# Third layer's first two blocks gathered ahead, in the last attention unit of a four-layer kernel

## The chip, the cores and the metric

One core of a Trainium2 chip runs the whole program in one launch. The metric is device time in microseconds (us) of one execution; it is given as the median of several runs. A profile comes from one further execution, whose own time is named beside its span.

## The reference, cut to what matters

Two images of 256 channels and 64 x 64 pixels go through four layers, all in fp32:

- layer 0: group norm, then attention with 4 heads over the 4096 pixels, a projection, and the sum with the normalised input;
- layer 1: a position term, linear in the pixel's place, is added;
- layer 2: a bottleneck (1x1 convolution to 64 channels, a deformable 3x3 convolution with mask, 1x1 back to 256, residual, relu);
- layer 3: twice (group norm, relu, deformable 3x3 convolution of 256 channels whose offsets come from a 7x7 depthwise and a 1x1 convolution), and the residual.

A deformable convolution samples, for each pixel and each of 9 taps, the image at a place of its own:

```python
y0 = jnp.floor(py); x0 = jnp.floor(px)
out = gather(y0, x0) * (wy0 * wx0) + gather(y0, x0 + 1) * (wy0 * wx1) \
    + gather(y0 + 1, x0) * (wy1 * wx0) + gather(y0 + 1, x0 + 1) * (wy1 * wx1)
```

The text speaks of the "second layer" (the bottleneck, layer 2) and the "third layer" (the deformable pair, layer 3), as the program's names do.

## The kernel before, in words

**Tiling.** An image is cut into 8 blocks of 512 pixels (8 rows). Each engine but SyncE executes its instructions in the order in which the Python code emits them (`manual_schedule`), so the loops below are the schedule; SyncE's DMAs are ordered by the framework. Each engine, SyncE's queue too, is in order: an instruction that waits holds all behind it.

**Attention** (`attention`). Four units (image b, pair of heads hp), each of 256 steps `n`; 16 steps are a block of 256 query pixels, so there are 64 attention blocks. A step issues scores (L569), the minimum (L581), exponentials (L587), transposes (L599) and products with the values (L628). `Block` holds what follows a block: `product` copies the products to the tile `o` (L460, one buffer), `spread` sends the shares through DRAM (`share_d` L495, two loads `f` L499), `combine` multiplies and adds on POOL (L508, L509, L514), `fetch` loads `res` (L203) and `project` projects (L533), stores `xa` (L546). Tile pools: `xp` 4, `kp` 5, `vp` 6 buffers. Small work is run from `due` times and from generators in the list `back`; `background` lets a generator take a step when no due work stands there: `bott.before` (second layer: 1x1, image to DRAM, offsets, corner indices and weights), `bott.conv(0)` and `early_image` (batch 0 of the second layer, its group norm, its output `xn` and gather image `img3[0]` in DRAM). `bott.before(1)` runs in the last unit and ends after it.

**Gathers.** `gather` (L817) is an indirect DMA on POOL's queue: 128 indices fetch the four corners of 128 pixels for one tap, a row of 4 KB each for the third layer (`four`, 512 KB) and 1 KB for the second (`bfour`). `offsets` makes a block's offsets: 14 matmuls into `pd` (L777), a copy `wide` (L788), 7 shifted matmuls (L794), a copy `od` (L803), 4 selections (L808), and `corners` (L722 to L760), which makes the indices `idx` and the weights `w4`.

**Third layer** (`deform`). 4 passes (two images, two convolutions) of 8 blocks of 36 steps `s`, 1152 in all: step `s` is one tap `k` and one quarter `j` of a block's pixels. A step issues the gather of step s + 8 (ten buffers in `gp`), the first corner of step s + 1 on ScalarE (`first`, L1328), the other three on DVE (`others`, L1334, three instructions), two transposes (L1346), every fourth step an evacuation (L1355), and one of the products with the weights (L1365). `Side` objects run generators beside the steps, at so many calls a step: the offsets of the blocks to come (24 calls for 36 steps), the `image` of the next pass, and `seconds`, which is `bott.conv(1)`, the second layer's batch 1. That has 144 units of two gathers, two calls each (DVE: `weigh` L1020, `add` L1030 and L1031; transposes L1041, products L1051 and L1073, output L1076, L1082, L1083, store to `x2d` L1118); with 8 units gathered ahead and the last steps it is about 312 calls. It starts before step 0 with 20 calls and goes on at 312 / 180 = 1.73 calls a step. When it ends, the image of batch 1 starts at 1.15 calls a step.

Of the kernel before, what the change touches and what calls it, by code (L numbers as in the profile page):

```python
# [18 lines left out]
P = 128  # L19
# [5 lines left out]
EPS = 1e-5  # L25
DWK = 7


# [32 lines left out]
class Net:  # L61
    def __init__(self, ctx, tc, a, out):
# [23 lines left out]

        self.pos_d = dram.tile([C, HW], F32, name="pos_d")
        self.share_d = [dram.tile([16, P], F32, name=f"share_d{n}") for n in range(2)]

# [83 lines left out]
    def attention(self, bott):  # L173
# [5 lines left out]
        with ExitStack() as ctx:  # L179
# [20 lines left out]

            def block(src, i, pool=xp, name="xb"):
                t = pool.tile([P, 2, 512], F32, name=name)
                nc.sync.dma_start(t, rows(src)[:, :, 512 * i : 512 * i + 512])  # L203
                return t
# [185 lines left out]
            def plan_unit(u):  # L390
# [4 lines left out]
                def load(key, i, b):  # L395
                    x.setdefault(key, []).append(block(self.xn_d[b], i))

# [38 lines left out]
            class Block:  # L436
# [81 lines left out]
                def fetch(self):  # L518
                    b, hp = units[self.u]
                    i = self.i // 2  # L520
                    self.res = block((self.xn_d, self.xa_d)[hp][b], i, one, "res")
                    if hp == 0:
                        src = rows(Block.pos_d)[:, :, 512 * i : 512 * i + 512]
                        self.pos = one.tile([P, 2, 512], F32, name="pos")
                        nc.sync.dma_start(self.pos, src)
# [139 lines left out]
            while n < last + 4 or back or any(own.values()):  # L665
                u, d = divmod(n, per_unit)
                if d == 0 and u < len(units):
                    plan_unit(u)
                    if u == 0:
                        back.append(prepare(1))  # L670
                    if u == 1:
                        back.append(bott.before(0, bt, ps))
                    if u == 2:
                        back.append(first_batch())
                    if u == 3:
                        back.insert(0, bott.before(1, bt, ps))

                def small(at):
# [83 lines left out]

    def offsets(self, i, srcs, wt, bias, base, idx, w4, pool, ods, ps):

# [8 lines left out]
        for s, src in enumerate(srcs):  # L773
            for t in order:
# [4 lines left out]
                    lhsT=wt(s, t),  # L779
                    rhs=src[:, (y + r0) * W : (y + r1) * W],  # L780
                    start=(n == 0),
                    stop=(n == len(srcs) * size - 1),
                )
                n += 1
                yield

        wide = ods[i % 2]
        nc.scalar.copy(wide[:m, :, half : half + W], pd[:m].rearrange("p (r w) -> p r w", w=W))  # L788
        yield
        pz = ps([P, 512])  # L790
        sums = pz.rearrange("p (r w) -> p r w", w=W)
        for t in range(size):
# [7 lines left out]
            )  # L800
        yield
        od = pool.tile([P, 512], F32, name="od")
        nc.scalar.activation(od, pz, AF.Identity, bias=bias)  # L803
        yield

        pt = ps([P, 4, 32])
        for j in range(4):
            nc.tensor.matmul(  # L808
                pt[:, j, :], lhsT=od[:, j * P : (j + 1) * P], rhs=self.sel, start=True, stop=True
            )  # L810
        yield
        for _ in self.corners(i, pt, False, base, idx, w4, pool):
# [12 lines left out]
    class Bottleneck:  # L825
# [4 lines left out]
        GROUPS = [(0, 1), (2, 3), (4, 5), (6, 7), (8,)]  # L830
        CORNERS = 11

        def __init__(self, ctx, net):
# [3 lines left out]
            self.corner = ctx.enter_context(tc.tile_pool(name="bt_c", bufs=self.CORNERS))  # L837
            self.idx, self.w4 = {}, {}
            self.h, self.blocks, self.done = {}, [0] * B, set()
            self.w1 = wp.tile([P, 2, CM], F32, name="w1")  # L840
# [77 lines left out]
        def before(self, b, pools, ps):  # L918
# [20 lines left out]
            def offsets(i):  # L939
# [30 lines left out]
                for _ in range((1, 6)[b]):  # L970
                    yield False
                while len(self.idx) == self.CORNERS:
                    yield False
                pt = ps([P, 4, 32])
                for j in range(4):
# [6 lines left out]
                for _ in net.corners(i, pt, True, self.base, idx, w4, work):  # L982
                    yield "any"

            for i in range(NB):
# [143 lines left out]
    def early_image(self, bott, pools, ps):  # L1129
# [6 lines left out]
        for i in range(NB):  # L1136
# [11 lines left out]
            for g in range(2):  # L1148
# [15 lines left out]
                yield True  # L1164

    def deform(self, bott):

# [3 lines left out]
        tc, nc, a = self.tc, self.nc, self.a  # L1171
        with ExitStack() as ctx:
            wp = ctx.enter_context(tc.tile_pool(name="df_w", bufs=1))
            work = ctx.enter_context(tc.tile_pool(name="df_work", bufs=2))
            cp = ctx.enter_context(tc.tile_pool(name="df_c", bufs=4))
            gp = ctx.enter_context(tc.tile_pool(name="df_g", bufs=10))
            sp = ctx.enter_context(tc.tile_pool(name="df_s", bufs=8))
# [24 lines left out]
            def offset_weights(l):  # L1202
# [9 lines left out]
                for cb in range(2):  # L1212
                    nc.vector.tensor_tensor(
                        self.wf[:, cb],
                        dw[:, cb].unsqueeze(2).to_broadcast([P, T, 2 * K2]),
                        pw[:, cb].unsqueeze(1).to_broadcast([P, T, 2 * K2]),
                        ALU.mult,
                    )
                    yield
# [3 lines left out]
            def conv_weight(l, k):  # L1223

                src = a["dcw"][l].rearrange("(c p) o -> p c o", p=P)
                wc[k] = wp.tile([P, 2, C], F32, name=f"wc{k}")
                nc.sync.dma_start(wc[k], src[:, 2 * k : 2 * k + 2, :])

# [40 lines left out]
            IMAGE = 4 + 6 * NB + 1  # L1269
            corners = {}  # L1270

            def offsets(b, l):
                if b == 0:
                    yield from offset_weights(l)
                wf = self.wf
                for i in range(NB):
                    idx = cp.tile([P, 4, K2], I32, name="didx")
# [8 lines left out]
                        self.vec[:, V_PWB + l : V_PWB + l + 1],  # L1286
                        base, idx, w4, work, ods, pd,
                    )

            begun = offsets(0, 0)  # L1290
            next(begun)
            load(0, self.xn_d[0], wp)
            ods = [wp.tile([P, 8, W + DWK - 1], F32, name=f"wide{n}") for n in range(2)]
# [15 lines left out]
            def gather(s):  # L1309
                if s < ALL:  # L1310
                    n, i, k, j = parts(s)
                    b, l = layers[n]
                    fours[s] = gp.tile([P, 4, C], F32, name="four")
                    idx = corners[b, l, i][0]
                    self.gather(
                        fours[s].rearrange("p s c -> p (s c)"), self.img3[b], idx[:, j, k : k + 1]
                    )

# [87 lines left out]
            class Side:  # L1406


                def __init__(self, start, rate, steps):
                    self.start, self.rate, self.steps, self.count = start, rate, steps, 0  # L1410

                def follow(self, s):
                    while self.steps and self.count < self.rate * (s - self.start):
                        self.count += 1
# [7 lines left out]
            second = bott.conv(1, bott.pools(inner, 9), ps)  # L1422
            offs = [Side(-LEAD - 6, OFFS / BLOCK, begun)]
            for k in range(K2):
                conv_weight(0, k)
            for s in range(-LEAD - 6, 0):
                offs[0].follow(s + 1)
                if s % 3 == 0:
                    next(second)
            for s in range(AHEAD):  # L1430
                gather(s)
            first(0)

            seconds = Side(0, 312 / (5 * BLOCK), second)
            stats[0] = self.norm_stats()
            images = []
            for s in range(ALL + 12):
# [12 lines left out]
                if seconds:  # L1450
                    seconds.follow(s)
                    if not seconds.steps:
                        seconds = None
                        stats[1] = bott.stats[1]
                        inner.close()
                        images.append(Side(s, 1.15, image(*layers[1])))
                if s % LAYER == LAYER // 2 and 1 <= n < len(layers) - 1:
# [112 lines left out]
```

## Time and profile before

| | |
|---|---|
| median of 3 runs | 5334.04 us (5333.5 to 5345.14) |
| the profiled execution | 5333.18 us, span 5331.4 us |
| busy: PE, DVE, ACT, POOL | 4839.4, 4190.9, 2822.3, 2238.2 us (91, 79, 53, 42%) |
| DMA | 920.43 MB, mean 173 GB/s |
| last attention unit, its exponentials | 2207.2 to 2940.1 us |
| third layer, step 0 (L1328) | 3025.7 us |

Engines: PE is TensorE's matmuls, PEld its weight loads, DVE VectorE, ACT ScalarE, POOL GpSimd, SP SyncE. In a group's line stand the source line, engine, operation, tile written and tiles read, number of instructions, busy time and mean of one in ns, and behind a second bar the idle time before them with what ended it. "issue" means that the profile shows nothing that was waited for; "remote" and "another core or an unknown queue" mean that it names no releaser.

### The profile page before, as it was taken

To read this page: it belongs to the slowest core of one execution; us is meant where nothing else is said; L and a number is where in the kernel's file an instruction comes from. 1 tells how busy PE (TensorE), PEld (TensorE's weight loads), DVE (VectorE), ACT (ScalarE), POOL (GpSimd) and SP (SyncE) were. 2 spreads that over 40 slices of the span, in tenths; PEclk is the share of its full clock that TensorE was granted. 3 is DMA by queue.
4 is the path that set the end of the run, shared out by engine and by line. 5 is a ranking of instruction groups with operands and counts; after the bars stand their busy time and mean duration, and the time that the engine had idled before them with its cause. 6 is when DMAs were issued, how large, how long until landed. Compare 5 with 4: busy or idle time off the path is not lost.

```text
span 5331.4 us, 99714 instructions
## 1 busy us (share of the span) xinstructions
PE 4839.4 (91%) x38200; PEld 2655.5 (50%) x38200; DVE 4190.9 (79%) x7927; ACT 2822.3 (53%) x5221; POOL 2238.2 (42%) x2238
## 2 busy tenths in 40 slices
PE   8999999999999999999999655566999999999998
PEld 5555565555655555555565222233444444444443
DVE  6877868787678888687777466677999999999998
ACT  5676656666566666666677121223444444444443
POOL 0111101000027777461000566674566566666664
PEclk9999999999999999999999777788999999999999
DMA  5222121111213333233301566567999999999997
GB/s 170 63 89 61 41 69 35 49 29 45 61 55 94 96 94 103 85 97 103 92 25 35 185 189 203 185 201 249 356 315 333 351 350 348 341 386 344 346 347 286
DMA packets 347150, 920.43 MB, mean 173 GB/s; under 512 B 58717, under 2 KB 98459, under 8 KB 346671
## 3 DMA queue, kind: packets, MB, share of 16 engines
q0 software_dynamic: 194688, 683.85, 36.7%
q1 hardware_dynamic: 151438, 230.07, 14.0%
q8 instruction: 300, 4.92, 0.4%
q14 instruction: 180, 1.47, 0.1%
q10 hardware_dynamic: 544, 0.13, 0.0%
HBM read 815.90 MB, written 89.60 MB: 170 GB/s over the span
## 4 chain that ended last, share of the span: by engine, by line
PE 37%; DVE 13%; issue 6%; another core or an unknown queue 3%; ACT 3%; POOL 2%; DMA 2%; SPq 0%; DVEq 0%; ACTq 0%; POOLq 0%
PE out L1365 11%; DVE smp L1334 8%; PE pd L777 6%; PE av L628 5%; PE sc L569 5%; PE tt L599 3%; PE pt L1346 3%; POOL bfour L817 1%; DVE bfour L1020 1%; DVE low L581 1%; DMA four<-img,didx 1%; PE pd L794 1%; ACT st L1355 1%; ACT smp L1328 1%
## 5 line engine op out<-in xcount | busy, mean ns | idle before, releaser
L1334 DVE SCALAR_TENSOR_TENSOR smp<-four,dw,smp 128x256 f32<-128x256 f32 x3456 | 1611.6, 483 | 222.7 <-ACT smp L1328 94.6
L587 ACT ACTIVATE e<-sc,low 128x1024 f32<-128x1024 f32 x1024 | 1146.3, 1119 | 718.9 <-DVE low L581 700.5
L817 POOL DMA_INDIRECT four<-img,didx x1152 | 1153.2, 1001 | 723.6 <-DVE smp L1334 328.1
L1365 PE MATMUL out<-st,wc 128*128 128x512 f32 x2304 | 1239.8, 621 | 164.8 <-ACT st L1355 94.5
L581 DVE TENSOR_REDUCE low<-sc 128x1 f32<-128x1024 f32 x1024 | 1205.3, 1219 | 222.2 <-PE sc L569 212.9
L569 PE MATMUL sc<-k,qs 64*128 64x512 f32 x2048 | 997.5, 606 | 0.6 <-ACT e L587 0.3
L628 PE MATMUL av<-et,v 128*64 128x256 f32 x8192 | 994.9, 385 | 0.0
L569 PE MATMUL sc<-k,q 64*128 64x512 f32 x2048 | 978.9, 604 | 0.0
L508 POOL TENSOR_TENSOR o<-o,f 128x1024 f32<-128x1024 f32 x63 | 148.9, 2364 | 1863.6 <-DVE o L460 760.8
L599 PEld LDWEIGHTS tt<-ident,e 64*128 64x128 f32 x16384 | 651.3, 139 | 521.2 <-issue 270.2
L1355 ACT COPY st<-pt 128x1024 f32<-128x1024 f32 x288 | 291.2, 1011 | 930.5 <-PE pt L1346 627.9
L599 PE MATMUL tt<-ident,e 64*128 64x64 f32 x16384 | 727.3, 226 | 38.5 <-ACT et L618 23.4
L618 ACT COPY et<-tt 128x512 f32<-128x512 f32 x1152 | 658.2, 584 | 194.8 <-PE tt L599 164.3
L616 DVE COPY et<-tt 128x512 f32<-128x512 f32 x896 | 612.8, 684 | 153.5 <-PE tt L599 149.7
L1346 PEld LDWEIGHTS pt<-ident,smp 128*128 128x128 f32 x2304 | 320.1, 145 | 785.7 <-issue 489.3
L628 PEld LDWEIGHTS av<-et,v 128*64 128x64 f32 x8192 | 551.2, 137 | 304.0 <-issue 49.6
L817 POOL DMA_INDIRECT bfour<-img,bidx x576 | 577.4, 1002 | 269.7 <-issue 115.1
L1365 PEld LDWEIGHTS out<-st,wc 128*128 128x128 f32 x2304 | 393.3, 197 | 426.1 <-issue 273.4
L1346 PE MATMUL pt<-ident,smp 128*128 128x128 f32 x2304 | 460.0, 282 | 105.0 <-DVE smp L1334 81.7
L1328 ACT ACTIVATE smp<-four,dw 128x256 f32<-128x256 f32 x1152 | 512.8, 502 | 74.8 <-DMA four<-img,didx 55.2
L777 PE MATMUL pd<-x,wf 128*126 128x512 f32 (+2 forms) x896 | 455.5, 595 | 5.3 <-issue 5.0
L569 PEld LDWEIGHTS sc<-k,qs 64*128 64x128 f32 x2048 | 345.9, 188 | 218.3 <-issue 125.6
(165 smaller groups left out, 3353.4 us busy)
## 6 DMA issues: line engine op xcount, KB each, us to landing
f<-share_d SPq DMA_DIRECT2D x128, 256.0 KB
xb<-xn SPq DMA_DIRECT2D x55, 512.0 KB
img<-imgt SPq DMA_DIRECT2D x96, 256.0 KB
four<-img,didx POOLq DMA_INDIRECT x1152
xa<-res SPq DMA_DIRECT2D x32, 512.0 KB
xb<-in_x SPq DMA_DIRECT2D x20, 512.0 KB
bfour<-img,bidx POOLq DMA_INDIRECT x576
qs<-q SPq DMA_DIRECT2D x64, 128.0 KB
```

The source lines that it names most:

```text
L569: nc.tensor.matmul(s[:, j, :], lhsT=q[u, i // 2][int(h != j)][halves[j], at : at + P], rhs=k[u][c][halves[j], h, :], start=True, stop=True,)
L581: nc.vector.tensor_reduce(low, s, AX.X, ALU.max, negate=True)
L587: nc.scalar.activation(e.rearrange("p j n -> p (j n)"), s, AF.Exp, bias=blk.low[:, g, c : c + 1], accum_out=blk.sum[:, g, c : c + 1],)
L599: nc.tensor.transpose(pt[:, m, :], e[half, m // 4, m % 4 * P : m % 4 * P + P], self.ident[half, half],)
L616: nc.vector.tensor_copy(dst, pt)
L618: nc.scalar.copy(dst, pt)
L628: nc.tensor.matmul(now["av"][halves[h], :], lhsT=v[u][c][:, m, halves[h]], rhs=ets[j][:, m, h, :], start=(m == 0), stop=(m == 7),)
L777: nc.tensor.matmul(pd[:m, r0 * W : r1 * W], lhsT=wt(s, t), rhs=src[:, (y + r0) * W : (y + r1) * W], start=(n == 0), stop=(n == len(srcs) * ...
L817: self.nc.gpsimd.indirect_dma_start(out=dst, out_offset=None, in_=img, in_offset=bass.IndirectOffsetOnAxis(ap=idx, axis=0),)
L1334: nc.vector.scalar_tensor_tensor(smps[s], four[:, c], weight(s, c), smps[s], ALU.mult, ALU.add)
L1346: nc.tensor.transpose(pts[u][:, c, j * P : (j + 1) * P], smp[:, c * P : c * P + P], self.ident,)
L1365: nc.tensor.matmul(outs[ob], lhsT=wc[k][:, c, ob * P : ob * P + P], rhs=sts[u][:, c, :], start=(k == 0 and c == 0), stop=(k == K2 - 1 and ...
```

## The change

The offsets of the third layer's blocks 0 and 1 (first image, first convolution) are made by a new generator, `early_samples`, which is appended to `back` in the last attention unit. It takes buffers of the attention's pools (three of `xp` for the gathers; the fourth is handed to the attention's own loads through `held`; two of `vp` for rows of `xn`, one of `kp` for `wide`), makes the offsets with `offsets`, issues the 72 gathers, and stores each result from SyncE to a DRAM tile `samp_d`. In `offsets` the steps that fill a PSUM bank yield `"bank"`, on which `early_samples` goes on at once. A flag `bott.lock` keeps the corners of `before(1)` and of `early_samples` apart. In `deform` the first 72 steps load `four` from `samp_d`, steps 0 to 7 from POOL's queue and the others from SyncE; the first convolution's weights are loaded from POOL's queue; `gp` is allocated first. The second layer's 20 calls before step 0 go; `seconds` now has 0.9 calls a step and 2.5 more in each of the first 72 steps, and the image that follows it 0.9 in place of 1.15. The offsets' `Side` starts 72 steps later, with block 2.

```diff
+EARLY = 2
...
-    def offsets(self, i, srcs, wt, bias, base, idx, w4, pool, ods, ps):
+    def offsets(self, i, srcs, wt, bias, base, idx, w4, pool, wide, ps, odp=None, y0=0, later=lambda f: f()):
...
-                yield
+                yield "bank"
...
                     if u == 3:
                         back.insert(0, bott.before(1, bt, ps))
+                        back.append(self.early_samples(bott, bt, held, xp, vp, kp, ps))
...
-                while len(self.idx) == self.CORNERS:
+                while self.lock or len(self.idx) == self.CORNERS:
                     yield False
+                self.lock = True
...
+    def early_samples(self, bott, pools, held, xp, vp, kp, ps):
+        nc, a = self.nc, self.a
+        T, half = DWK * DWK, DWK // 2
+        xs = [vp.tile([P, 8, P], F32, name="v").rearrange("p m c -> p (m c)") for _ in range(2)]
+        src = self.xn_d[0].rearrange("(cb p) n -> p cb n", p=P)
...
+        xbs = [xp.tile([P, 2, 512], F32, name="xb") for _ in range(4)]
+        held.append(xbs.pop())
...
+        fours = deque(x.rearrange("p u n -> p (u n)") for x in xbs)
+        gathers, stores = deque(), deque()
+
+        def gather():
+            if stores:
+                nc.sync.dma_start(*stores.popleft())
+            if gathers:
+                dst, idx = gathers.popleft()
+                fours.rotate(1)
+                self.gather(fours[0], self.img3[0], idx)
+                stores.append((dst, fours[0]))
+
+        for i in range(EARLY):
...
+            for done in steps:
+                if done == "bank":
+                    continue
+                while bott.lock and not mine:
+                    yield False
+                bott.lock = mine = True
+                gather()
+                yield True
+            bott.lock = False
+            if i + 1 < EARLY:
+                load(i + 1)
+            while gathers:
+                gather()
+                yield True
+            for m in range(4 * K2):
+                k, j = divmod(m, 4)
+                gathers.append((self.samp_d[i][m * P : m * P + P, :], idx[:, j, k : k + 1]))
+        while gathers or stores:
+            gather()
+            yield True
...
+            gp = ctx.enter_context(tc.tile_pool(name="df_g", bufs=10))
             wp = ctx.enter_context(tc.tile_pool(name="df_w", bufs=1))
...
-                nc.sync.dma_start(wc[k], src[:, 2 * k : 2 * k + 2, :])
+                queue = (nc.gpsimd, nc.sync)[l]
+                queue.dma_start(wc[k], src[:, 2 * k : 2 * k + 2, :])
...
+                    if n == 0 and i < EARLY:
+                        queue = nc.gpsimd if s < AHEAD else nc.sync
+                        m = 4 * k + j
+                        queue.dma_start(four, self.samp_d[i][m * P : m * P + P, :])
+                        return
...
-                    while self.steps and self.count < self.rate * (s - self.start):
+                    while self.steps and self.count < self.rate * (s - self.start) + self.more(s):
...
-            offs = [Side(-LEAD - 6, OFFS / BLOCK, begun)]
-            for k in range(K2):
-                conv_weight(0, k)
-            for s in range(-LEAD - 6, 0):
-                offs[0].follow(s + 1)
-                if s % 3 == 0:
-                    next(second)
             for s in range(AHEAD):
                 gather(s)
+                conv_weight(0, s)
+            conv_weight(0, AHEAD)
+            begun = offsets(0, 0)
+            next(begun)
+            load(0, self.xn_d[0], wp)
+            offs = [Side(EARLY * BLOCK - LEAD - 6, OFFS / BLOCK, begun)]
             first(0)
 
-            seconds = Side(0, 312 / (5 * BLOCK), second)
+            seconds = Side(0, 0.9, second, lambda s: 2.5 * min(s, EARLY * BLOCK))
...
-                        images.append(Side(s, 1.15, image(*layers[1])))
+                        images.append(Side(s, 0.9, image(*layers[1])))
```

## The prediction

> **What bounds the kernel now.** I read the busy tenths of the 40 slices first, then the busy time by stretches, then the groups of instructions of the slow stretch, what one line of it did in time, and at last the chain of waits at the stretch's start and SyncE's timeline in the attention.
>
> ```profile
> PE   8999999999999999999999655566999999999998
> DVE  6877868787678888687777466677999999999998
> ...
> POOL 0111101000027777461000566674566566666664
> PEclk9999999999999999999999777788999999999999
> ```
>
> A slice is 133 us. From slice 23 to 28 (some 2950 to 3700 us) TensorE falls to half, its clock too, and POOL is at its highest. This is where the second layer's batch 1 runs beside the third layer's first blocks.
>
> ```profile
> 2599.70:2898.40 298.70, 297.32 (x3279) 178.93 (x3279) 220.10 (x348) 210.29 (x396) 30.48 (x21) 1.00 0.11 32
> ...
> 3011.00:3322.00 311.00, 167.54 (x523) 73.16 (x523) 199.18 (x469) 64.00 (x120) 215.96 (x213) 0.76 0.63 201
> 3322.00:3670.00 348.00, 207.18 (x672) 94.85 (x671) 239.86 (x555) 81.89 (x154) 231.09 (x225) 0.78 0.61 195
> ...
> 3848.00:5086.00 1238.00, 1174.19 (x4212) 570.97 (x4211) 1140.89 (x2690) 559.31 (x1043) 749.89 (x754) 0.99 0.95 345
> ```
>
> Columns: stretch, length, busy PE, PEld, DVE, ACT, POOL, clock, DMA share, GB/s. The last attention unit (first row) is TensorE's: 297 of 299 us, POOL idle, DMA at 0.11. The slow stretch (rows two and three) has no full engine: POOL 447 of 659, DVE 439. In the last row TensorE, DVE and DMA are all above 0.9: no room there.
>
> ```profile
> L817 POOL DMA_INDIRECT bfour<-img,bidx x288 | 293.4, 1019 | 184.4 <-issue 73.3 <-DVE bsmp L1031 58.4 <-DVE pos L731 20.0
> L1334 DVE SCALAR_TENSOR_TENSOR smp<-four,dw,smp 128x256 f32<-128x256 f32 x459 | 222.1, 484 | 100.2 <-ACT smp L1328 56.7 <-issue 14.4 <-ACT bst L1043 7.1
> ...
> L817 POOL DMA_INDIRECT four<-img,didx x162 | 166.3, 1026 | 49.4 <-issue 45.7 <-ACT smp L1328 1.8 <-ACT bst L1043 0.6
> ...
> L1020 DVE TENSOR_TENSOR bfour<-bfour,bw 128x512 f32<-128x512 f32 x137 | 93.7, 684 | 0.3 <-issue 0.3
> ...
> L1030 DVE TENSOR_TENSOR bfour<-bfour 128x256 f32<-128x256 f32 x137 | 57.6, 421 | 4.1 <-remote 1.7 <-DVE bfour L1020 0.7
> ...
> L1031 DVE TENSOR_TENSOR bsmp<-bfour 128x128 f32<-128x128 f32 x136 | 39.8, 293 | 20.3 <-remote 7.0 <-issue 2.2 <-DVE bfour L1030 1.5
> ...
> L1328 ACT ACTIVATE smp<-four,dw x162: 490/506/532, 3025.7 to 3660.1; 128x256 f32<-128x256 f32 x162
> ```
>
> A gather holds POOL for 1.02 us, and the next starts 0.30 us after it for "issue" (45.7/150): 1.32 us each. From the first gather after the start-up (3010.5) to the end of the second layer's work (about 3665) POOL issues some 268 `bfour` and 171 `four`, 439 x 1.32 = 580 of 655 us: the stretch goes 1.13 times slower than POOL alone would. The last row gives a step of the third layer (one gather's worth) as 634.4/162 = 3.92 us. After the stretch 830 steps take 1365 us, 1.645 each. So every step that leaves the POOL-paced stretch saves 2 us.
>
> ```profile
> by line: issue 20.1%; another core or an unknown queue 16.0%; DVE smp L1334 13.4%; DVE bfour L1020 5.7%; POOL bfour L817 5.4%; PE out L1365 4.2%; PE pd L777 3.5%; DMA four<-img,didx 3.2%; DVE bfour L1030 3.1%; POOL four L817 2.1%; PE pt L13
> ...
> 2989.47 13.82 PE pd L777 x28
> ...
> 3004.00 1.98 PE pd L794 x12
> ...
> 3006.75 1.09 PE pd L808 x8
> ...
> 2636.50 0.36 SPq L546 DMA_DIRECT2D xa<-res  x1
> 2640.92 0.36 SPq L203 DMA_DIRECT2D res<-xa  x1
> 2647.47 0.32 SPq L495 DMA_DIRECT2D share_d<-shares  x1
> ...
> 2649.64 1.12 SPq L499 DMA_DIRECT2D f<-share_d  x2
> ```
>
> The chain from 2900 to 3700 us, its pieces at the start, and SyncE in the attention. 16% of the chain (some 125 us) has no named releaser: ScalarE waits on TensorE (`bst` L1043, longest 30.8 us) while TensorE has its matmuls started and does not report them done. That speaks against POOL as the only bound.
>
> **The change, part by part.** By the built programs' order, both early blocks' offsets stand in the attention's block 56 of 64 and the 72 early gathers in blocks 56 to 62, as 10, 10, 13, 10, 13, 10, 6 between POOL's `combine` calls; none is left over at the end.
>
> *Attention, TensorE.* Two blocks of offsets: 28 pd matmuls 13.8 us, 14 shifts at 0.165 = 2.3, 8 selections 1.1: 17.2 us, all exposed, since the unit is TensorE's. DVE (two filters of 1.07 us, 30 small operations of 0.2) and ScalarE (four copies of 0.6) have 26 to 30% free and cost nothing. The same matmuls leave the slow stretch, where TensorE is half idle and only the first 20 us of them (2989 to 3009) were on the chain.
>
> *Attention, queues.* Each gather's store waits on SyncE for the gather, and three buffers rotate; behind the stores in SyncE's order stand `share_d`, `f`, `res` and the `xb` loads, and behind the gathers in POOL's order stands `combine`. `combine` must end before DVE's next copy to `o`, which has 3.5 us to spare (2617.5 to 2621.0). A round trip: gather to use 4.4 us (four(0) issued 3021.34, used 3025.70), store 4.4 (2636.50 to the dependent load at 2640.92), 0.4 issue: 9.2 us for three gathers. SyncE's room from one `f` to the next `share_d` is 38.7 us; a group of 13 needs about 15.4 + 3R, one of 10 15.4 + 2R (11 us to the end of `combine`, R the round trip, 4.4 for the last landing). R = 9.2 gives 43 and 34: late by 1 us twice. With `f` and others on the same DMA engines I take R = 12: 51.4 and 39.4 against 38.7 + 3.5, late 2 x 9.2 less what the 10-groups give back, 7 us. Bounds: R = 8, nothing; R = 15, 2 x 18.2 + 4 x 3.2 = 49. Attention: +24 us.
>
> *Start of the third layer.* Step 0 no longer waits for offsets and gathers: it can start when batch 1's last corners end (ScalarE's last L729 at 2984.9), not at 3025.7. POOL first issues 8 loads, 9 weights, dw, pw and x: 23 x 0.65 = 15 us from 2950, which ends before the second layer's first gather (2975, held by `img`): nothing.
>
> *Steps 0 to 72.* No step gathers on POOL; the second layer's rate of 3.4 calls a step brings 117 of its 144 units by step 72 (DVE's order shows the same), so 250 `bfour` gathers. 18 are issued while DVE finishes the corners; 232 x 1.32 = 306 us. DVE: 216 x 0.484 + 117 x 1.398 + 6.5 blocks x 3.85 (L1076, L1082, L1083 twice each) + 10 = 303 us. Two engines are level, so I take 1.2 where POOL alone had 1.13: 365 us. Bounds 1.1 and 1.4: 333 and 424.
>
> The loads are 37.7 MB beside 39 MB of others, 77 MB in 365 us, 211 GB/s: the stretch ran 195 to 201 GB/s at a DMA share near 0.62, so DMA still fits, and SyncE's waits for x2d stores (4.4 us) are covered by ten buffers, some 40 us. The Trainium skill ("DMA: Bandwidth & Descriptors", "Issuing engines are not separate DMA queues") speaks against the change: moving a DMA to another issuer saves only its issue time, because all share 16 DMA engines. If DMA were the bound, the detour through DRAM would save nothing in this stage and the sum would end near no change; here the issue time is the price that the row shows.
>
> *Steps 72 to 128.* 27 units remain. DVE: 56 x 1.45 + 27 x 1.4 + 13 = 132 us; POOL 94 x 1.32 = 124. DVE leads; x 1.15 = 152 us (135 to 180).
>
> *Steps 128 to 180.* The image of batch 1 at 0.9: 52 x 1.81 (steps 168 to 228 before: 3696 to 3805) = 94 us.
>
> *Sum.* Before: step 180 at 3720.8. After: 2985 + 365 + 152 + 94 = 3596, less by 125. The image is over at step 196 and not at 226: 30 x 0.165 = 5 less. Attention +24. Total -106 us on the profiled execution's 5333.2 us (span 5331.4), 0.9 below the runs' median of 5334.0: 5227 us.
>
> **The rivals.** *DVE and the unnamed holds become the bound (slower).* In the slow stretch DVE's wall time is 659/439 = 1.50 of its busy time. If the holds come with time or with the second layer's units, not with gathers, steps 0 to 128 cost 1.5 x (303 + 132) = 653 and step 180 comes at 2985 + 653 + 94 + 24 = 3756, with the image -5: +30 us, 5363. It decides from a ratio of 1.43. For it: no engine is full there, 16% of the chain is unnamed. Against: POOL explains 580 of 655 us, and part of the 1.50 is DVE waiting for POOL's gathers.
>
> *The early chain paces the attention (slower at its end).* It would need 112 us of slip: 14R - 161 = 112, R = 19.5 us, twice the rows. At R = 15 the time is 5269.
>
> *Half of it.* A ratio of 1.3 gives 565 + 94: step 180 at 3668 with the attention, -58 us, 5275.
>
> **How the numbers follow.** Forecast near 1.2: 0.68; ratio about 1.3 or a slip of 40 to 50 us: 0.17; ratio 1.43 and more: 0.11; R above 19: 0.04. Low end: 333 + 135 and no slip, -56: 5172, rounded to 5175. High end: the ends +59, +28, +42 not all at once (root of squares 78) give 5305, and r = 1.38 gives 5310. Three tenths of a percent, 16 us, is about what can be told from no change (the runs spread over 0.2%). Faster 0.85, same 0.05, slower 0.10.
>
> **What would show it.** Right: last attention unit longer by 20 to 30 us; first step near 3010; steps 0 to 72 in 330 to 420 us with DVE and POOL both above 80%; step 180 near 3620; steps after it at 1.65. Wrong: DVE's copy to `o` waiting on POOL in blocks 57 to 63; unnamed holds as large as before in a shorter stretch; DVE waiting for `four` loads queued on SyncE.

## The result, and the profile after

The changed kernel takes 5328.82 us (median of 22 runs, 5314.62 to 5342.85), the kernel before beside it 5340.94 us (22 runs, 5331.58 to 5359.74): ratio 0.9974, 95% interval 0.9964 to 0.9983. The forecast was 5227 us with a range from 5175 to 5310; the gain is 12 to 14 us, not 106. The profiled spans stand at 5331.4 and 5325.1 us.

First the slices of the page (tenths of busy time, 133 us each).

```profile
PE   8999999999999999999997856568999999999998
DVE  6877868787678878677664668768898999999998
...
POOL 0111101000027777462122267665666566666665
PEclk9999999999999999999998957789999999999999
```

The three slices from 2530 to 2930 us, inside the attention, have POOL at 1, 2 and 2 where it was 0, and in the last of them TensorE falls from 9 to 7 and its clock to 8. The slice after it, where before the third layer began, now holds the attention's end (TensorE 8, was 6). By stretches:

```profile
2603.30:3043.70 440.40, 380.70 (x3812) 222.67 (x3811) 258.73 (x435) 244.54 (x455) 102.69 (x96) 0.93 0.59 202
3090.10:3446.90 356.80, 204.97 (x594) 90.98 (x595) 268.54 (x614) 72.54 (x136) 246.87 (x235) 0.72 0.62 202
3446.90:3622.00 175.10, 111.49 (x365) 50.29 (x363) 123.17 (x288) 48.03 (x91) 113.96 (x110) 0.83 0.67 218
...
3646.80:3728.90 82.10, 76.16 (x287) 39.00 (x286) 76.29 (x182) 41.08 (x74) 44.55 (x45) 0.98 1.01 385
```

Columns as in the prediction. The first row is attention blocks 56 to 63: TensorE was busy for 297 of 299 us in a stretch of seven such blocks before; now it stands idle for 60 of 440, and its granted clock is 0.93. Rows two and three are steps 0 to 72 and 72 to 128 of the third layer. The last is steps 137 to 180, where no second-layer gather is left: the DMA engines are full (share 1.01).

The terms of the sum, from the first instruction of each kind in the two traces (first pair of kernels), and from a second pair of profiles on a chip of another kind, which the experiments explain:

| term (us) | forecast | first pair | second pair (b1, a1) |
|---|---|---|---|
| last attention unit, first to last exponential | +24 | 731.8 to 834.1: +102 | 733.3 to 830.0: +97 |
| last exponential to step 0 | -41 | 86.7 to 46.3: -40 | 85.5 to 46.3: -39 |
| steps 0 to 180 | -84 | 695.0 to 638.8: -56 | 612.4 to 573.9: -38 |
| steps 180 to 228 (image) | -5 | 83.9 to 77.3: -7 | 81.2 to 76.8: -4 |
| everything else | 0 | -5 | +3 |
| sum (profiled spans) | -106 | -6 | +18 |

So the forecast failed in the attention by 78 us, and in the third layer by 28.

The attention, first TensorE's own rows (start, duration, engine, line):

```profile
2605.68 11.00 PE L796 MATMUL pm<-v,bx 128*126 128x512 f32 x28
2621.78 1.95 PE L816 MATMUL pm<-k,shift 126*32 126x512 f32 x14
...
2641.82 12.28 PE L796 MATMUL pm<-v,bx 128*126 128x512 f32 x28
```

Two rows of x28, one for each early block. A block has 14 fp32 matmuls here, so the trace holds two records for each (shown in e8). Then one group of ten gathers, from POOL's, SyncE's, VectorE's and TensorE's timelines (in brackets the idle time before, and what ended it):

```profile
2701.74 0.94 POOL L839 DMA_INDIRECT xb<-img,bidx  x1 [0.30 <-issue]
2710.35 0.94 POOL L839 DMA_INDIRECT xb<-img,bidx  x1 [7.67 <-DMA samp_d<-xb]
...
2733.80 0.94 POOL L839 DMA_INDIRECT xb<-img,bidx  x1 [6.71 <-DMA samp_d<-xb]
2745.92 2.34 POOL L516 TENSOR_TENSOR o<-o,f 128x1024 f32<-128x1024 f32 x1 [11.18 <-DMA f<-share_d]
```
```profile
2703.22 34.90 SPq L1232 DMA_DIRECT2D samp_d<-xb  x10
2738.22 0.38 SPq L503 DMA_DIRECT2D share_d<-shares  x1
2740.64 1.76 SPq L507 DMA_DIRECT2D f<-share_d  x2
```
```profile
2750.44 0.42 DVE L468 COPY o<-av 128x256 f32<-128x256 f32 x1 [6.94 <-POOL avs L522]
```
```profile
2751.51 1.11 PE L607 MATMUL tt<-ident,e 64*128 64x64 f32 x15 [5.33 <-DVE et L624]
2752.56 3.67 PE L636 MATMUL av<-et,v 128*64 128x256 f32 x16
```

The ten gathers go out in threes, 11 us apart, and need 35.5 us (2699.2 to 2734.7). SyncE issues its ten stores in 34.9 us and only then `share_d`, then `f`; `combine` starts at 2745.9, VectorE's copy to `o` waits 6.9 us for it, and TensorE 5.3 us for VectorE. A group of 13 ends the same way with 15.5 us. Behind this pause the products with the values take 3.67 us instead of 1.95, behind the other pauses of the last blocks 3.3 to 3.7: the clock is at half.

### The profile page after: what moved, and what is told of

Read it like the earlier page. It is cut to its first block, busy times and chain, and to the rows that moved or that the text cites. A ratio compares the mean times of both kernels' runs of the same rounds, so it can differ in the third digit from the quotient of the medians.

```text
span 5325.1 us, 100018 instructions
## 1 busy us (share of the span) xinstructions
PE 4862.2 (91%) x38200; PEld 2662.4 (50%) x38200; DVE 4193.1 (79%) x7929; ACT 2829.3 (53%) x5221; POOL 2261.7 (42%) x2256
## 3 DMA queue, kind: packets, MB, share of 16 engines
q1 hardware_dynamic: 169438, 300.73, 17.2%
## 5 line engine op out<-in xcount | busy, mean ns | idle before, releaser
L1440 DVE SCALAR_TENSOR_TENSOR smp<-four,dw,smp 128x256 f32<-128x256 f32 x3240 | 1504.0, 483 | 166.5 <-ACT smp L1434 68.6
L839 POOL DMA_INDIRECT four<-img,didx x1080 | 1086.4, 1006 | 695.1 <-DVE smp L1440 286.3
L839 POOL DMA_INDIRECT bfour<-img,bidx x576 | 588.2, 1021 | 226.3 <-issue 106.6
L1434 ACT ACTIVATE smp<-four,dw 128x256 f32<-128x256 f32 x1080 | 482.3, 502 | 67.6 <-DMA four<-img,didx 44.1
L796 PE MATMUL pd<-x,wf 128*126 128x512 f32 x840 | 435.7, 601 | 0.0
```

The costliest lines, as they stand in the source:

```text
L796: nc.tensor.matmul(pd[:m, r0 * W : r1 * W], lhsT=wt(s, t), rhs=src[:, (y + r0 - y0) * W : (y + r1 - y0) * W], start=(n == 0), stop=(n == l ...
L839: self.nc.gpsimd.indirect_dma_start(out=dst, out_offset=None, in_=img, in_offset=bass.IndirectOffsetOnAxis(ap=idx, axis=0),)
L1440: nc.vector.scalar_tensor_tensor(smps[s], four[:, c], weight(s, c), smps[s], ALU.mult, ALU.add)
```

## The experiments

All comparisons below are of kernels run beside each other on one chip. The chips are of two kinds: on one the kernel before takes 5341 to 5342 us (the first pair, b0, a0, e5, e6), on others 5194 to 5201 us (all others). All six profiles of the first kind show "holds": ScalarE and VectorE wait, up to 30.8 us at a time, in front of instructions that read TensorE's results, and the profile names no releaser ("remote"). The twelve profiles of the other kind show none. So ratios are compared, and stretches of the same kind of chip. The slip is the last unit's length, first to last exponential, less 732.5 us, the mean of three profiles of the kernel before (731.8, 732.4, 733.3). Some of its spread lies in blocks 48 to 55, ahead of the early work (389 to 399 us there); over blocks 56 to 63 alone the changed kernel's three profiles slip by 101, 102 and 100 us, e1 by 34, e2 and e9 by 50 and 51, e7 and e12 by 38 and 35.

**Without the early gathers (e1).** The offsets stay.

```diff
-                gathers.append((self.samp_d[i][m * P : m * P + P, :], idx[:, j, k : k + 1]))
...
-                        queue.dma_start(four, self.samp_d[i][m * P : m * P + P, :])
+                        rows = self.img3[0][m % 16 * 256 : m % 16 * 256 + 256, :]
+                        queue.dma_start(four, rows.rearrange("(p t) f -> p (t f)", t=2))
```

> The changed kernel without the 72 early gathers and their 72 stores; the offsets stay in the attention, and the third layer's first 72 loads read rows of the gather image in order instead of samp_d (left out: the two blocks' gathers, so the output is not the reference's). Last exponential of the last attention unit: 2939.0 us in the kernel before, 3043.7 in the changed one, a slip of 104.7. Theory Q (the slip is mostly the chain of gathers, stores, f and combine): the offsets' own 33 to 36 us of slip stay and some 68 go; the total falls by about 68 from the changed kernel's 5329, to 5260 (5250 to 5275), and the wait of POOL at combine for f is back near the kernel before (four waits of 38.7 us in the window of the last blocks). Rival T (the slip is work on TensorE and the two other engines that the two blocks of offsets bring, and the queues only show it): the slip stays at 90 to 105 us and the total within 10 us of the changed kernel's.

Measured: slip 33, all of it in block 56; ratio 0.9912 (0.9895 to 0.9928). Theory Q holds: of 97 to 109 us of slip the gathers make about two thirds, 64 to 76 (65 to 68 by blocks 56 to 63), and the offsets 33. The expected 5260 us was for the first kind of chip. The waits of POOL at `combine` are long again, since POOL is early:

```profile
POOL o L516 <- DMA f<-share_d: 110.4, 3, 37.7
```

(engine, line, what it waited for, us in total, times, longest; last blocks of e1).

**Eight buffers (e2), and a cap of ten gathers between two `combine` (e7, e12).**

```diff
-        wide = kp.tile([P, 2, 512], F32, name="k").rearrange("p u n -> p (u n)")
+        spare = [kp.tile([P, 2, 512], F32, name="k").rearrange("p u n -> p (u n)")] + xs
...
+            spare.append(t)
...
                 load(i + 1)
+            else:
+                fours.extend(spare)
```

> The changed kernel with eight buffers instead of three for the early gathers, once the second block's offsets are done (the buffers of wide, of the two row tiles and of the two filter tiles join the rotation). Theory Qb (the round trip through three buffers, some 11 us for every three gathers, makes the 13 gathers of a group outlast a block): most of the slip after block 57 goes, 40 to 60 us, total 5270 to 5290. Rival Qo (the order decides: f stands behind the stores on SyncE, and combine behind the gathers on POOL, each store waiting for its own gather's landing): a group's end moves by a few us only, slip 85 to 105, total within 15 us of the changed kernel's 5329. Rival D (DMA's bandwidth): no change either, but gathers and stores get longer with eight in flight.

Measured: slip 52, ratio 0.9939 (0.9922 to 0.9955), so Theory Qb and neither rival; in a second run of it, e9, slip 51 and 0.9938 (0.9920 to 0.9956).

> The eight-buffer kernel once more, beside the cap of ten and beside the kernel before on this chip. Slip 52 us as before on any chip. On a chip with the unnamed holds the third layer gains 97 to 104 us up to step 180, so total 40 to 52 below the kernel before, ratio 0.990 to 0.992; on a chip without them 0.9939, as before.

In POOL's waits of the last blocks, the time in which a gather waits for a store of its buffer falls from 161.9 us in the changed kernel to 25.4 (`xb`; with the other tiles 50):

```profile
POOL xb L839 <- DMA samp_d<-xb: 161.9, 29, 8.8
```
```profile
POOL xb L839 <- DMA samp_d<-xb: 25.4, 8, 7.3
```

So the round trip through three buffers is the larger part of the queues' share: 45 to 57 of 64 to 76 us. What stays are two pauses of TensorE, in the two blocks with 13 gathers. The cap takes them away: a counter `room`, set to 10 by `combine` and lowered by each gather, at 0 holds the generator back.

```diff
+                    bott.room = 99 if end else 10
...
+                bott.room -= 1
...
+            while bott.room <= 0:
+                yield False
             gather()
             yield True
```

> Eight buffers, and at most ten gathers between two calls of combine (10, 10, 10, 10, 10, 10, 10 and the last 2 after block 63, in place of 10, 10, 13, 10, 13, 10, 6). With eight buffers, only blocks with 13 gathers still stalled (5.3 and 9.5 us longer, two pauses of TensorE of 3.5 and 6.8 us). Theory Q (a block holds ten round trips beside its f, but not thirteen): these two pauses go, slip of the last attention unit 34 to 40 us (52 with eight buffers alone, 102 to 109 in the changed kernel), total 12 to 18 us below the eight-buffer kernel's. If the pauses have another cause than the size of the group: slip 48 to 56, total as the eight-buffer kernel's.

Measured: slip 38, no pause above 2.7 us; ratio 0.9907 (0.9891 to 0.9924), 10 us below the eight-buffer kernel where 12 to 18 were expected. Run again as e12: slip 33 (36 to 40 expected), ratio 0.9919 (0.9906 to 0.9933).

> The eight-buffer kernel with the cap of ten again. Slip 36 to 40 us. On a chip without holds ratio 0.9907 again (0.989 to 0.9925). On a chip with holds the third layer's gain of 97 to 104 stays whole against the slip of 38, and 5 us are given back at the image: 54 to 66 us below the kernel before, ratio 0.9875 to 0.990.

The cap is as good as leaving the gathers out (e1), and it is the best version that computes the whole. On the first kind of chip it was not run. It also shows that the DMA engines' bandwidth was not the limit: in the attention's last 365 us e12 makes the same gathers and stores at a higher DMA share (0.67; 0.59 in the changed kernel), with TensorE busy for 360 us:

```profile
2592.50:2957.20 364.70, 359.88 (x3762) 212.72 (x3760) 256.28 (x428) 239.94 (x449) 102.70 (x96) 1.00 0.67 243
```

**`share_d` and `f` from ScalarE's queue (e3), and with eight buffers (e4).**

```diff
-                    nc.sync.dma_start(d, t)
+                    queue = nc.scalar if self.u == 3 and self.i >= 8 else nc.sync
+                    queue.dma_start(d, t)
...
-                        nc.sync.dma_start(
+                        queue.dma_start(
```

> The changed kernel with share_d and f of the last attention unit's blocks from 56 on issued on ScalarE's queue, not on SyncE's, where they stand behind the early gathers' stores. Theory Qo (f behind the stores on SyncE): the waits of POOL's combine for f in the last blocks (five waits of 15.7 us, 65 in all) fall to below 20 in all, the slip falls from 105 to some 40 to 60 us, and the total to 5270 to 5290; ScalarE loses 1 to 4 us a block while it waits for the shares. Rival Qp (combine stands behind the ten or thirteen gathers on POOL, whatever f does): the f waits vanish but DVE's copy to o waits as long for POOL, slip 85 to 105, total within 15 us of 5329.

> Eight buffers and ScalarE's queue together. If the slip beyond the offsets' 33 to 36 us is the chain of round trips and order, whichever part has more of it, both parts go: slip 33 to 45, total 5258 to 5275, about 1.1 to 1.5 per cent below the kernel before. If something else holds the attention (DMA bandwidth, POOL's time for 72 gathers): slip above 70 and total above 5300.

Measured: e3 slip 93, ratio 1.002 (1.001 to 1.003); e4 slip 64, ratio 0.9962 (0.9952 to 0.9973), worse than eight buffers alone. For e3 the number is that of rival Qp, but not its mechanism: VectorE's copy to `o` no longer waits for POOL. And e4 missed its expectation by some 20 us. What takes the f wait off POOL puts it on ScalarE, which now waits in front of its next exponentials, three times for 49.6 us in all, with a store to `samp_d` as the releaser, and TensorE's pauses (five, of 4.4 to 18.7 us) end with ScalarE:

```profile
POOL xb L840 <- DMA samp_d<-xb: 148.3, 26, 8.3
```
```profile
ACT e L596 <- DMA samp_d<-xb: 49.6, 3, 22.6
```
```profile
2781.46 1.22 PE L578 MATMUL sc<-k,qs 64*128 64x512 f32 x1 [16.63 <-ACT e L596]
```

(e3, lines moved by one.) So the edit moved a wait, and these two runs do not tell what SyncE's order by itself costs. The Trainium skill says that moving a DMA to another issuer saves only its issue time ("DMA: Bandwidth & Descriptors", "Issuing engines are not separate DMA queues"), which the prediction held against the change. The number here agrees: the move brought 4 us of slip (97 to 93, same kind of chip), and cost 11 in e4. The reason that the trace shows, ScalarE's instructions held behind the DMAs on its own queue, is not in that section.

**One tap in place of 14 (e8).** It decides how much of the 33 us in block 56 is TensorE's work.

```diff
+        if odp:
+            srcs, order = srcs[:1], [half]
...
-                    stop=(n == len(srcs) * size - 1),
+                    stop=(n == len(srcs) * len(order) - 1),
```

> The changed kernel with one matmul into pd for each of the two early blocks instead of 14 (left out: 13 of 14 taps, so the offsets of these two blocks and the output are not the reference's). By the changed kernel's rows the 14 take 11.0 us for one block. Theory T2 (those rows are real TensorE time, for one block each): block 56 is 2 x 13/14 x 11 = 20 us shorter than in the changed kernel, +33 becomes +12 to 14, and the slip 102 to 109 becomes 82 to 90. Rival T1 (28 records are the matmuls of both blocks, as the prediction took it, and the rest of the 33 us is waiting): +33 becomes +20 to 25.

Measured: block 56 is 14.2 us longer than before, not 32.7 to 34.3, and the slip is 84. 19 to 20 us for 13/14 of two blocks' matmuls: Theory T2, a row of x28 is one block. The row of the one matmul that is left has two records:

```profile
2589.51 1.12 PE L798 MATMUL pm<-v,bx 128*126 128x512 f32 x2
```

**One block ahead (e6).** `EARLY = 1`, eight buffers, second layer at 1.73 calls a step and 1.67 more in the first 36.

> One block gathered ahead instead of two (36 gathers), with eight buffers from the end of its offsets, and the second layer at 1.73 calls a step plus 1.67 in each of the first 36 steps. By the terms as the first runs give them: the attention's slip is one block of offsets, 17 us, and half of the eight-buffer kernel's other 19, together 22 to 30 (53 with two blocks); the third layer up to step 180 gains half of what two blocks gain, 40 to 50; total 15 to 25 us below the kernel before, ratio 0.995 to 0.997, and above the eight-buffer kernel's 0.9939. If the fixed part of the change (first layer's start without offsets before step 0, the second layer's pace) is most of the gain: ratio 0.991 to 0.993.

Measured: slip 44, last exponential to step 180 742 us (782 in b0, 678 in a0), ratio 0.9995 (0.9981 to 1.0009), where 0.995 to 0.997 was expected. The third layer's gain is 40 of 104 us, the low end of what was expected. The slip was expected at 22 to 30. Two pauses of TensorE, of 6.2 us in block 56 and 5.9 us in block 58, are most of the rest: each stands behind a hold of this kind of chip, which here fell into the attention, 7.1 and 6.8 us long:

```profile
ACT et L626 <- remote: 13.9, 2, 7.1
```

The pauses and the half clock behind them make some 16 us; without them the slip would be about 27 us, as expected (an estimate; e6 was not run on the other kind of chip).

**The kernel before and after once more (b0, a0; b1, a1).**

> The kernel before, unchanged, for its profile beside the experiments' own chip. The first profiles (kernel before and changed kernel) show unnamed holds of TensorE's results, up to 30 us each, in the second layer's batch 1; the profiles of the first experiments show none. Theory H (the holds belong to that chip or moment, not to the kernel): this profile shows no unnamed releaser of over 3 us between the attention's end and step 180, and that stretch is 40 to 60 us shorter than the 770 us of the first profile (2950.5 to 3720.8), some 715 to 730. Rival K (the holds come from the kernel's second layer at its old place, and the experiments avoided them by their pace): the holds are there, and the stretch stays above 755.

> The changed kernel, unchanged, beside the kernel before on the same chip. By the first timing its ratio is 0.9974. Theory H: the attention's slip (last exponential 102 to 105 us later than in the kernel before, both from the unit's start) is the same on this chip, since no hold lies in it; the third layer up to step 180 is 80 to 97 us shorter than in the kernel before; ratio 0.996 to 1.003. Rival K: holds also here, ratio as the first.

> The kernel before, for its profile. On a chip without the unnamed holds (total near 5198): no unnamed releaser from the attention's end to step 180, and that stretch takes 680 to 700 us (by the experiments' steps 228 to 1151, counted back from the total), against 781 on the chips with holds. On a chip with holds (total near 5341): 781 again.

> The changed kernel beside it. The slip of the last attention unit is 102 to 109 us on any chip. On a chip without holds the stretch from the last exponential to step 180 takes 615 to 625 us, a gain of only 60 to 85, so the change makes the kernel slower there: 20 to 40 us, ratio 1.003 to 1.008. On a chip with holds 0.9974 again. If the holds have nothing to do with the gain: ratio 0.996 to 0.999 on either.

b0 and a0 fell on the first kind of chip: last exponential to step 180 782 and 678 us, slip 109, ratio 0.9974 (0.9962 to 0.9986), as in the first pair. b1 and a1 fell on the other kind: 698 and 620 us, slip 97 (102 to 109 was expected), and the change makes the kernel slower there, ratio 1.0041 (1.0027 to 1.0055), inside what was expected. The holds go with the kind of chip and not with the kernel: the first row below is from the kernel before in the first pair; in b1, the same kernel, no wait is marked "remote", and its longest sum is one for gathers' landings.

```profile
ACT bst L1043 <- remote: 109.7, 9, 30.8
```
```profile
ACT smp L1328 <- DMA four<-img,didx: 359.8, 132, 18.6
```

What a hold is stays open, and so does whether it belongs to the chip or to its state at that hour; where there are none, steps 0 to 180 of the kernel before are 83 us shorter. So the expectation for b0, that the stretch would be shorter there, missed with the chip, and b1 met it.

**Less VectorE (e11), on the cap of ten.**

```diff
-                    for c in range(1, 4):
+                    for c in range(1, 2 if s < EARLY * BLOCK else 4):
```

> The eight-buffer kernel with the cap of ten, with one of the three weighted sums of VectorE left out... that is, only the second corner is added in steps 0 to 71 (left out: the third and fourth corner of these steps, so the output is not the reference's). VectorE loses 144 x 0.484 = 70 us of its some 270 in that stretch. Theory P (POOL's gathers at 1.32 us pace steps 0 to 72): the stretch gets shorter by less than 20 us of its 303 (chip without holds) or 355 (with holds). Rival V (VectorE is the bound, or POOL's pace is VectorE's through its buffers): shorter by 45 to 70 us.

Steps 0 to 72, e12 and then e11:

```profile
3003.40:3307.20 303.80, 199.96 (x600) 91.23 (x600) 268.51 (x610) 72.73 (x136) 232.37 (x222) 0.76 0.69 228
```
```profile
3004.40:3301.00 296.60, 189.65 (x600) 86.94 (x600) 205.97 (x471) 72.59 (x136) 226.21 (x222) 0.80 0.71 233
```

VectorE loses 63 us, the stretch 7. Theory P: POOL paces it, 222 gathers at 1.32 us, 293 of 304 us. This is the kind of chip without holds; on the other it was not run.

**The second layer's pace (e5, e10).** In e5 the old 1.73 calls a step (and the image's old 1.15), in e10 (on the cap) 0.9 + 3.5.

```diff
-            seconds = Side(0, 0.9, second, lambda s: 2.5 * min(s, EARLY * BLOCK))
+            seconds = Side(0, 312 / (5 * BLOCK), second)
...
-                        images.append(Side(s, 0.9, image(*layers[1])))
+                        images.append(Side(s, 1.15, image(*layers[1])))
```

> The changed kernel with the second layer's old pace (312/180 = 1.73 calls a step from step 0, none extra in the first 72 steps, and the image of batch 1 at 1.15). The early gathers stay. Theory M (POOL's 1.32 us a gather paces these stretches, so what counts is the sum of gathers up to step 180, not their order): steps 0 to 72 get shorter by a third (302 to 357 us to about 210 to 240), steps 72 to 180 longer by the same, and the total is within 12 us of the changed kernel's. Theory W (where there are no gathers of the third layer, the pace that fills POOL is what brings the gain): steps 0 to 72 are limited by DVE and the loads instead and save only 40 to 60 us, later steps go at the old 3.9 us each, and the total is 25 to 60 us above the changed kernel's.

> The cap of ten, and the second layer at 0.9 + 3.5 calls a step in the first 72 steps (all of its 144 units beside the steps that do not gather, in place of 117). POOL: 288 gathers less 18 at 1.32 us = 356 us for steps 0 to 72; DVE 216 x 0.484 + 144 x 1.4 + 40 = 346. Theory M (POOL's gathers pace the stretch, wherever they stand): steps 0 to 72 in 360 to 430 us, steps 72 to 180 in 185 to 215, together as with the cap alone within 15 us, total within 15 us of it. Theory W (units beside loads are cheaper than beside gathers): steps 0 to 180 together 20 to 45 us shorter than with the cap alone. If POOL and DVE, both near full, hold each other up: 20 to 50 us longer.

Measured: e5 207 + 447 us for steps 0 to 72 and 72 to 180, a0 355 + 277; ratio 1.0004 (0.9992 to 1.0016), 19 us above a0, between the two theories. e10 401 + 187 us, e7 305 + 271; ratio 0.9922 (0.9905 to 0.9938), 5 us above e7 beside it: Theory M. The changed kernel's pace is near the best of the three; what counts is the number of gathers before step 180, not much their order.

## Why the prediction was wrong, step by step

*Attention, TensorE (17.2 us forecast): mis-sized.* The step "28 pd matmuls 13.8 + 14 shifts 2.3 + 8 selections 1.1: 17.2 us" took a row of the kernel before, x28 in 13.82 us, for two blocks. It is one block. The rows above give 11.0 + 12.3 + 2 x (1.95 + 1.08) = 29.3 us, e8 confirms it, and e1 shows 33 us of slip for it: the rest is a pause of 2.6 us in block 56 and, in e1, the half clock behind it.

*Attention, queues (7 us forecast, 0 to 49): the step that failed most.* The round trip was taken at R = 12 us and is 11 (2699.21, 2710.35, 2721.86). But the formula, "a group of 13 needs about 15.4 + 3R, one of 10 15.4 + 2R", counts one round trip too few. Every gather of a group is issued behind one `combine` and stored ahead of the next `f`, so ten gathers in threes need three full waits and thirteen four: 15.4 + 3R and 15.4 + 4R, with R = 11.2 some 49 and 60 us against the 42.2 of room, 7 late for a group of ten and 18 for one of 13. Blocks 58 to 62 of the first pair, behind groups of 10, 13, 10, 13 and 10, were 7.7, 18.3, 10.9, 18.2 and 12.9 us longer; the first group of ten fell into block 56, which the offsets make longer anyway, and came in time. The pauses of TensorE alone are 5.3, 15.5, 7.4, 15.7 and 10.3, 54 us. Of the other 14 the clock makes some 11: after the five restarts it stands at 0.50 for 4.6, 3.7, 6.0, 4.4 and 4.1 us, 22.8 in all, and half of that is lost. Two rows of the changed kernel, the pause of 15.5 us and what follows (clock in the third column from the end):

```profile
2803.60:2815.50 11.90, 0.00 (x0) 0.00 (x0) 0.00 (x0) 0.00 (x0) 4.19 (x3) 0.51 0.65 178
2815.50:2820.90 5.40, 3.70 (x29) 2.47 (x31) 5.07 (x12) 2.62 (x5) 2.99 (x4) 0.50 0.56 171
```

TensorE starts again at half its clock. The Trainium skill states this ("TensorE: Matmul & The Clock Gate", Part 1: half rate after an idle window of about 3.4 us, full rate after about 3.4 us of work). The rows of this profile agree in kind for pauses of 5.3 us and more, with 3.7 to 6.0 us until full rate. But a shorter pause does it too: all fifteen profiles with early offsets have the same pause of 2.63 us in block 56, and behind it the products took 1.95 us in five (the first pair's among them) and 2.9 to 3.7 in ten, as in a0:

```profile
2638.94 0.71 PE L607 MATMUL tt<-ident,e 64*128 64x64 f32 x15 [2.63 <-DVE et L624]
2639.58 3.53 PE L636 MATMUL av<-et,v 128*64 128x256 f32 x16
```

The forecast priced a pause by its length alone.

*Start of the third layer (-40.7): right*, 40.4 and 39.2.

*Steps 0 to 72 (365 us): right*, 357 and, without holds, 304. POOL's 1.32 us a gather is what e11 shows. The surcharge of 1.2 came out by luck: the forecast took it because POOL and VectorE were level, but without holds the factor is 1.04 (304 to 293), so that on the first kind of chip it goes with the holds, 53 us. With e11 one half of the first rival, VectorE as the bound, fell; the other half, the holds, is this difference.

*Steps 72 to 128 (152, bounds 135 to 180): 174.5*, inside its bounds, 165 without holds: 62 + 60 gathers in a1, 161 us at 1.32. The forecast counted 94, 54 for 27 units and so only 40 of the third layer's own, where the traces have 57 and 60. The 22 us above the forecast are the largest part of the third layer's 28.

*Steps 128 to 180 (94): mis-sized*, 107 and 106. It was priced at 1.81 us a step from a stretch of the kernel before. 9 of the 13 us lie in steps 128 to 137, 25.4 us for nine steps: the forecast had the second layer done by step 128, but VectorE's last sum for it starts at 3632.1, in step 130, and its last output is stored in step 139. The other 4 lie in the 43 last steps (137 to 180), which take 1.91 us each, on full DMA engines (the row with share 1.01), where POOL would need 44 x 1.32 = 58 us for its gathers of 82.

In steps 0 to 180 POOL issues 445 gathers in the kernel before and 397 in the changed one, on both kinds of chip. 48 x 1.32 = 63 us is, as an estimate, what the change can bring there; 56 came in the first pair and 38 without holds, where the full DMA engines of steps 137 to 180 took 24 back. With the 40 us of the start, the third layer's gain is 78 to 104 us, and a slip of 97 to 109 takes it back: the early chain paces the attention, as the second rival said, though at R = 11 and not at the 19.5 that it was given. It was priced with the same formula.

## What to carry to other kernels

Work that is hidden in a stage with an idle queue still passes that stage's own chain: count, for each block, what stands ahead of the block's critical DMA on its queue and ahead of its critical instruction on the engine: as many full round trips as the operations divided by the buffers, rounded up, less one, and then the last one's landing. If the count does not fit the block, more buffers and a cap on what goes between two critical instructions give back nearly everything that the queues cost (slip 97 to 109 us, 52 with eight buffers, 33 to 38 with the cap, of which 33 is TensorE's own work); here another issuing queue did not. The count is not the whole: with eight buffers a group of 13 fits by it, and its blocks were still 5 to 10 us longer. Before a price per operation is taken from a row, check how many records the trace writes for one instruction.

## What the runs showed of the hardware

- An fp32 matmul of 512 columns leaves two records (x2 for one in e8); 14 matmuls take 11.0 to 12.3 us.
- TensorE's clock after a pause of 5.3 us or more is 0.50 for 3.7 to 6.0 us of work (five pauses of the first pair); such a pause costs some 2.8 us beyond its length (14 us in all, 11 of them the clock's). A pause of 2.63 us halved the clock in ten of fifteen profiles.
- Chips differ by 2.7% on this kernel (5341 against 5194 to 5201 us). On the slower kind, instructions that read TensorE's results wait for up to 30.8 us with no named releaser, most of them between the attention's end and step 180; the cause is open. A change worth -0.3% on one kind is +0.4% on the other, so the sign of a small change belongs to a kind of chip.
